# A four-layer graph network on one core: a new order of the stage of adj, ACT issuing a store, units of up to three chunks, and one norm from row sums

## The chip, the cores and the metric

The kernel runs on one core of a Trainium2 chip. The metric is the device time of one execution in microseconds (us). The engines are called PE (TensorE, matrix products), DVE (VectorE), ACT (ScalarE), POOL (GpSimd, which here gathers and scatters rows by DMA) and SP (SyncE, which here issues DMAs). Every engine has its own stream of instructions, in an order that is fixed when the kernel is built. Where an engine needs the result of another it waits on a semaphore, and everything behind the waiting instruction on that engine waits too.

## The reference

There are N = 3327 nodes with D = 512 features (x, fp32), and an adjacency matrix adj of 3327 x 3327 int32, in which about 0.12% of the entries are one: some four neighbours a row. Four layers follow, each of them x = x + layer(relu(norm(x))):

```python
# layer 0: mean over the neighbours
agg = mask @ h / max(deg, 1)
out = relu(concat(h @ W_self + b_self, agg @ W_nb + b_nb) @ W_comb + b_comb)
# layer 1: graph attention with 8 heads of 64
Wh = h @ W[head];  e = leaky_relu(f_src[i] + f_dst[j]), masked by adj
out = softmax(e) @ Wh
# layer 2: the same with 4 heads of 512/4 inputs expanded to quaternion weights, then elu
# layer 3: one head of 512:  out = softmax(e) @ (h @ W.T)
```

norm takes the mean and variance over the 512 features of a row, without learned scales.

## The kernel before, in words

The rows are handled in 26 chunks of 128 nodes. The kernel uses how sparse adj is: it builds a list of the neighbours of each row once, and each layer then gathers the rows of the neighbours from a table in DRAM. A general path without lists exists and is not taken with these inputs.

**Stage of adj** (lines 852 to 1513). SP loads adj in 52 halves of a chunk into four buffers (ai). DVE searches each half for its ones (FIND_INDEX, L1209), ACT counts them with a Square whose sum it keeps (L1217). In the same stage the weights are loaded; W_self and W_nb of layer 0 are multiplied with the halves of W_comb on PE (L976) and copied out as wf (L989 by ACT, L987 by DVE). The chunks of x are loaded, normed and turned (hT, copied by ACT at L1342), and two products per chunk follow (L1349): pz, the part that the neighbours will need, which ACT copies to zt (L1358, L1361) and SP stores to the table of layer 0 (L1366), and py, the part of the row itself. At the end the rows are sorted by their number of neighbours: 26 scatters of POOL (L1435) put the own rows into the sorted order, and a read brings back the sorted records (srec).

**Layers 0 to 3.** After the sort the chunks differ in how many neighbour slots they have: 14, 8, 7, 7, 6, 6, 6, 5, 5, 5, 5, 4 (five times), 3 (five times), 2 (three times), 1, 1 for chunks 0 to 25, 117 in all. For a chunk, POOL gathers one slot after the other (L1562, one indirect DMA of up to 128 rows) into a ring of 33 slots. Layer 0 sums the slots, on PE with an identity matrix (L1593) and on DVE (L1887, L1895); layers 1 and 2 compute attention weights (L1941 to L1978), multiply the slots with them on DVE (L2110) or, for as many slots as ON_ACT says, on ACT (L2096), and sum on PE and DVE (L2138). L2148 adds the result of layer 1 to xres, which stays in SBUF. Then `project` prepares the next layer for the same chunk: mean and variance (bn_stats and its aggregate on DVE, L1649 and L1650, or, where SUMMED is true, from row sums: the update at L2148 keeps the sum of its result, DVE turns it into a mean at L1617, ACT squares the centred row and keeps that sum at L1625), an inverse root (L822, L824 on ACT, L831 to L836 on DVE), relu on ACT (L1676), transposes on PE (L1694), copies on ACT (L1705), the product with the weights on PE (L1780; L1737 is a small additional one of layer 3), and copies out (L1803 to L1806), which SP stores to the next table (L1764, L1822). A next layer may gather only when the whole table is stored: POOL waits for it at a small memset, the mark (L2194). Layer 3 makes its products after the gathers: weighted sums on DVE (L2030), transposes (L2046), the product with W and the addition of xres on PE (L2060, L2058), a copy on ACT (L2067), and a scatter on POOL of the finished rows to the output (L2072), which stands in POOL's stream between the gathers.

**The order of the work.** The instructions of each engine are put in order when the kernel is built, by a list scheduler (class Plan). Every operation has an engine, a planned cost and a rank. The scheduler takes the operation that can start first by these planned costs and, where several can, the one with the lowest rank. `limits` gives the number of buffers of each kind that it may count on. In the stage of adj the rank follows the planned times that ORDER_W, WORK, WORK0, X0, X and SELF set (when the weights are due, when the chunk of x, and how late a chunk's py may be). In a layer the rank follows ORDERS: a tuple of units for each layer, each unit one or more chunks that share the small operations of norm and softmax. POOL gathers the units in this order.

```python
ORDERS = {
...
    3: (
        (0,), (7,), (17,), (15, 20), (25,), (11,), (3,), (23,), (1, 5), (24,), (4, 14), (16,), (12, 22), (8,),
        (9,), (10,), (18,), (2,), (13,), (19,), (21,), (6,),
    ),
}
ON_ACT = {
    1: {S: min(S // 3, 1) for S in range(1, SLOTS + 1)},
    2: {S: S // 5 for S in range(1, SLOTS + 1)},
}
SUMMED = {1: False, 2: False, 3: False}
```

Of the kernel before, what the change touches and what calls it, by code (L numbers as in the profile page):

```python
# [18 lines left out]
P = 128  # L19
# [7 lines left out]
def general_path(  # L27
# [519 lines left out]
    def l3_finish(pc, i, o):  # L547
# [15 lines left out]
SLOTS = 16  # L563
# [46 lines left out]
ORDER_W = {1: -20.0, 0: -1.0, "bias": -4.0, "later": 20.0}  # L610
ADJ, WORK, WORK0, X0, X, SELF = 1.0, 1.13, 1.2, -14.0, 1.77, 7.0
# [81 lines left out]
def gnn_stack_kernel(  # L693
# [41 lines left out]
    with ExitStack() as st:  # L735
# [82 lines left out]
        def rough(pool, tag, var, scale=1.0):  # L818

            n = var.shape[-1]  # L820
            ln = pool.tile([P, 2], F32, tag="ln", name=f"ln{tag}", bufs=3)[:, :n]
            nc.scalar.activation(ln, var, AF.Ln, bias=eps, scale=scale)  # L822
            r0 = pool.tile([P, 2], F32, tag="r0", name=f"r0{tag}", bufs=3)[:, :n]
            nc.scalar.activation(r0, ln, AF.Exp, bias=lift, scale=-0.5)  # L824
            return r0

        def refined(pool, tag, mv, r0):

            n = r0.shape[-1]
            a = pool.tile([P, 2], F32, tag="nra", name=f"nra{tag}", bufs=3)[:, :n]  # L830
            nc.vector.scalar_tensor_tensor(a, r0, -1.0, r0, ALU.mult, ALU.mult)  # L831
            nc.vector.scalar_tensor_tensor(a, mv[:, :, 1], EPS, a, ALU.add, ALU.mult)
            r = pool.tile([P, 2], F32, tag="rs", name=f"rs{tag}", bufs=3)[:, :n]
            nc.vector.scalar_tensor_tensor(r, a, 3.0 * LIFT * LIFT, r0, ALU.add, ALU.mult)
            nmr = pool.tile([P, 2], F32, tag="nmr", name=f"nmr{tag}", bufs=3)[:, :n]
            nc.vector.scalar_tensor_tensor(nmr, mv[:, :, 0], -1.0, r, ALU.mult, ALU.mult)  # L836
            return r, nmr

        def refined_sums(pool, tag, mv, r0):

            n = r0.shape[-1]
            a = pool.tile([P, 2], F32, tag="nra", name=f"nra{tag}", bufs=3)[:, :n]
            nc.vector.scalar_tensor_tensor(a, r0, -1.0 / D, r0, ALU.mult, ALU.mult)
            nc.vector.scalar_tensor_tensor(a, mv[:, :, 1], D * EPS, a, ALU.add, ALU.mult)
            r = pool.tile([P, 2], F32, tag="rs", name=f"rs{tag}", bufs=3)[:, :n]
            nc.vector.scalar_tensor_tensor(r, a, 3.0 * LIFT * LIFT, r0, ALU.add, ALU.mult)
            nmr = pool.tile([P, 2], F32, tag="nmr", name=f"nmr{tag}", bufs=3)[:, :n]
            nc.vector.tensor_tensor(nmr, mv[:, :, 0], r, ALU.mult)
            return r, nmr


        with tc.tile_pool(name="p0", bufs=1) as pa, tc.tile_pool(name="p0p", bufs=2, space=PSUM) as pp:
# [444 lines left out]
            for p0 in range(0, NK, 2):  # L1297
# [25 lines left out]
                for j, i in enumerate(unit):  # L1323
# [41 lines left out]
                    def store(i=i, key=key):  # L1365
                        nc.sync.dma_start(table[0][i * P : (i + 1) * P, :D], tiles["zt", key])  # L1366

                    rows_in.append(load(rank, 4.0 * P * D, store, (), [o2], give=("zt",)))
# [147 lines left out]
        with tc.tile_pool(name="run", bufs=1, reuse_waits="tile") as pr, tc.tile_pool(  # L1516
# [7 lines left out]
            limits = {"xy": 3, "acc": 2, "pt": 2, "pw": 2, "h": 3, "hT": 3, "t": 3, "neg": 2, "ee": 2, "y": 3}  # L1524
# [77 lines left out]
            def project(layer, unit, updated, rank):  # L1602
# [233 lines left out]
            def summing(layer, unit, j):  # L1836
# [3 lines left out]
                if j == 0:  # L1840
                    new("mv", (layer, unit[0]), [P, 2, 2])
# [418 lines left out]
```

## Time and profile before

| | |
|---|---|
| median of three runs | 1074.55 us (1073.38 to 1076.67) |
| profiled execution | 1231.77 us |
| its span | 1230.0 us |
| mean granted PE clock in it | 0.855 |
| busy in the span: PE, DVE, ACT, POOL | 901.8, 726.6, 518.2, 610.1 us |
| stage of adj, then sort | 0 to 268, 268 to 278 us |
| layer 0, 1, 2, 3 | 278 to 514, 514 to 759, 759 to 998, 998 to 1230 us |
| first and last gather, layer 0 | 278.2, 458.1 us |
| layer 1 | 518.6, 719.9 us |
| layer 2 | 763.8, 961.4 us |
| layer 3 | 999.3, 1201.5 us |

The profile is one execution on the chip taken by the hardware profiler; the median comes from other executions of the same program. The profiled one is 157 us longer than the median. "Busy" is time in which an engine executes; the loading of weights into PE overlaps its products and is counted apart (PEld). A line such as L1562 is a line of the kernel. A wait is written as the waiting instruction, an arrow, and the instruction that ended the wait, then the sum in us, the number of waits and the longest. The stages above are bounded by POOL's marks at 514.2, 759.5 and 998.4 us.

### The profile page before, as it was taken

The numbers are of one execution on the slowest core, as the hardware profiler recorded it, in microseconds if no ns is written. First come the engines' busy times: TensorE is split into PE (matmuls) and PEld (weight loads), VectorE is DVE, ScalarE is ACT, GpSimd is POOL, SyncE is SP. The second block draws the span as 40 slices with busy tenths as digits, with TensorE's granted clock in tenths as the row PEclk, the third lists the DMA queues.
The fourth block names the chain that finished last, engine by engine and source line by source line (L and its number), as shares of the span: only waits on it lengthen the run. The fifth ranks groups of instructions, "written<-read, shape, count | busy, mean of one in ns | idle before, by whom it ended". The sixth has DMA issues, their size and how long they took to land. (4 is left out here: it accounts for less than half of the span.)

```text
span 1230.0 us, 11605 instructions
## 1 busy us (share of the span) xinstructions
PE 901.8 (73%) x2853; PEld 510.4 (41%) x2853; DVE 726.6 (59%) x1848; ACT 518.2 (42%) x1700; POOL 610.1 (50%) x719
## 2 busy tenths in 40 slices
PE   7599999854098889752979796539979832948865
PEld 4244444322075656531647464214435421423322
DVE  6499989204176557453869784628894815534441
ACT  4488886210043433422656553316554621312221
POOL 1064246717655550175757511766883236675661
PEclk9899999977599899966989889659896956978987
DMA  9999894958587772265666521665754345575561
GB/s 352 338 364 338 294 306 146 317 203 286 172 268 252 247 249 89 76 195 149 198 183 178 154 79 55 189 187 150 209 169 129 91 121 149 168 206 160 163 186 59
DMA packets 89910, 240.49 MB, mean 196 GB/s; under 512 B 24933, under 2 KB 26477, under 8 KB 89834
## 3 DMA queue, kind: packets, MB, share of 16 engines
q0 software_dynamic: 41600, 137.72, 38.1%
q1 hardware_dynamic: 48234, 101.96, 23.3%
q8 instruction: 24, 0.39, 0.1%
q14 instruction: 52, 0.43, 0.1%
HBM read 190.35 MB, written 49.27 MB: 195 GB/s over the span
## 5 line engine op out<-in xcount | busy, mean ns | idle before, releaser
L1562 POOL DMA_INDIRECT ring<-table,nbr x351 | 368.5, 1050 | 185.5 <-issue 80.9
L1593 PE MATMUL acc<-ring,ident 128*128 128x512 f32 (+1 forms) x494 | 266.6, 676 | 66.8 <-DVE ring L2110 24.3
L1780 PE MATMUL pw<-w,hT 128*128 128x264 f32 (+1 forms) x832 | 197.3, 394 | 18.3 <-ACT hT L1705 13.6
L1780 PEld LDWEIGHTS pw<-w,hT 128*128 128x128 f32 x832 | 161.2, 195 | 60.9 <-ACT hT L1705 20.5
L1593 PEld LDWEIGHTS acc<-ring,ident 128*128 128x128 f32 (+1 forms) x494 | 98.7, 215 | 175.1 <-issue 107.5
L1562 POOL DMA_INDIRECT ring<-table,srec x117 | 110.1, 941 | 77.8 <-issue 31.5
L2110 DVE TENSOR_TENSOR ring<-ring,w 128x2048 f32<-128x2048 f32 (+7 forms) x76 | 114.3, 1531 | 4.7 <-DVE w L1978 3.0
L2060 PE MATMUL pw<-w,hT 128*128 128x512 f32 x208 | 101.7, 634 | 13.3 <-ACT hT L2052 11.0
L1209 DVE FIND_INDEX8 fidx<-one_i,ai 128x8 uint32<-128x832 int32 x104 | 104.2, 1018 | 0.0
L1349 PE MATMUL pz_n<-wf,hT_n 128*128 128x512 f32 x208 | 95.2, 609 | 10.9 <-ACT hT_n L1342 8.4
L1705 ACT ACTIVATE hT<-pt 128x128 f32<-128x128 f32 (+1 forms) x312 | 81.8, 292 | 39.7 <-PE pt L1694 18.5
L1217 ACT ACTIVATE junk<-ai 128x1664 int8<-128x1664 int32 (+1 forms) x52 | 82.7, 1590 | 32.6 <-DMA ai<-in_adj_dram 32.2
L1694 PE MATMUL pt<-ident,h 128*128 128x128 f32 x208 | 36.5, 312 | 75.9 <-ACT h L1676 73.4
L1349 PE MATMUL py_n<-wf,hT_n 128*128 128x512 f32 x208 | 91.9, 592 | 0.0
L1803 ACT COPY t<-pw 128x512 f32<-128x512 f32 (+1 forms) x54 | 30.6, 566 | 134.0 <-PE pw L1780 43.9
L1941 DVE TENSOR_TENSOR e<-ring,fs 128x24 f32<-128x24 f32 (+25 forms) x96 | 15.2, 172 | 120.2 <-DMA ring<-table,nbr 102.0
L2060 PEld LDWEIGHTS pw<-w,hT 128*128 128x128 f32 x208 | 42.3, 207 | 73.2 <-issue 51.3
L1705 ACT ACTIVATION_READ_ACCUMULATOR hT<-pt 128x1 f32 x312 | 69.5, 223 | 0.0
L1694 PEld LDWEIGHTS pt<-ident,h 128*128 128x128 f32 x208 | 28.1, 160 | 96.3 <-ACT h L1676 81.6
L2194 POOL MEMSET mark<- 1x1 f32 x3 | 0.3, 88 | 132.7 <-DMA table<-t 132.7
L1349 PEld LDWEIGHTS pz_n<-wf,hT_n 128*128 128x128 f32 x208 | 39.8, 195 | 62.8 <-issue 49.4
L2046 PE MATMUL pt<-ident,y 128*128 128x128 f32 x96 | 16.4, 312 | 67.4 <-issue 56.8
(185 smaller groups left out, 1319.7 us busy)
## 6 DMA issues: line engine op xcount, KB each, us to landing
ai<-in_adj_dram SPq DMA_DIRECT2D x25, 832.0 KB
ai<-in_adj_dram SPq DMA_DIRECT2D x25, 831.5 KB
table<-t SPq DMA_DIRECT2D x52, 258.0 KB
xy<-own SPq DMA_DIRECT2D x26, 512.0 KB
table<-t SPq DMA_DIRECT2D x26, 260.0 KB
table<-zt_n SPq DMA_DIRECT2D x26, 256.0 KB
ring<-table,nbr POOLq DMA_INDIRECT x351
later<-in_x_dram SPq DMA_DIRECT2D x15, 256.0 KB
```

What stands on the lines that cost most here:

```text
L1209: nc.vector.max_index(fidx[:, i, qq * 8 : (qq + 1) * 8], one_i, ai[:, q * QW : min(cols, (q + 1) * QW)])
L1217: nc.scalar.activation(junk[:, :cols], tiles["ai", key][:, :cols], AF.Square, accum_out=sq[:, i, hf : hf + 1])
L1349: nc.tensor.matmul(pz, tiles["hT", key][:, c, :], wf[s][:, c, :], start=(c == 0), stop=(c == DC - 1))
L1562: nc.gpsimd.indirect_dma_start(out=ring[:m, r0 + s, : width[layer]], out_offset=None, in_=table[layer], in_offset=bass.IndirectOffsetOnAxi ...
L1593: nc.tensor.matmul(acc, ident[:m, :], g[:m, s, :D], start=(k == 0), stop=(k == len(slots) - 1))
L1694: nc.tensor.transpose(pt[:, c, :], h[:, c * P : (c + 1) * P], ident)
L1705: nc.scalar.activation(hT[:, c, :n], pt[:, c, :n], AF.Copy, accum_out=hsum[layer][:, i, c : c + 1])
L1780: nc.tensor.matmul(pw[:, b, :w], tiles["hT", key][:, c, :], wsb[layer][:, c, b, :w], start=(c == 0), stop=(c == DC - 1),)
L1803: nc.scalar.copy(t[:, :D].rearrange("p (b f) -> p b f", b=2)[:, lo:hi, :], pw[:, lo:hi, :HD])
L2046: nc.tensor.transpose(pt[:, c, :], tiles["y", key][:, c * P : (c + 1) * P], ident)
L2060: nc.tensor.matmul(pw[:, 0, :], tiles["hT", key][:, c, :], w3[:, c, :], start=False, stop=(c == DC - 1))
L2110: nc.vector.tensor_tensor(v, v, box["w"][:m, j, lo:hi, :].unsqueeze(3).to_broadcast([m, hi - lo, H, O]), ALU.mult,)
```

## The change

All of it changes the order of the work or the engine that does it; what is computed stays.

- The store of zt to the table of layer 0 is issued by ACT instead of SP (26 stores); the plan counts 0.35 us of ACT for it. ORDER_W, WORK, WORK0, X0, X and SELF have new values, and the plan counts 1.5 instead of 2.0 us for the landing of each scatter of the own rows. In the resulting order of SP ten chunks of x instead of eight are loaded ahead of W_self, and W of layer 3 before the third half of adj.
- ORDERS is new for all layers. Layers 0 to 3 had 22, 19, 19 and 22 units of one or two chunks and have 23, 22, 18 and 18 of one to three. Small tiles shared by a unit have three columns instead of two.
- The rules of ON_ACT for layers 1 and 2 are exchanged: layer 1 multiplies 12 slots on ACT instead of 21, layer 2 21 instead of 12.
- SUMMED is true for layer 2. That norm is computed in the stage of layer 1: 26 bn_stats with their aggregates leave DVE, 22 small centring operations come to it, the 26 updates of L2148 keep a sum, and ACT gains 26 Squares that keep a sum.
- The scheduler counts on one buffer instead of two for neg and two instead of three for y.

```diff
 ORDERS = {
     0: (
-        (24,), (12, 21), (11,), (6,), (18,), (17,), (15,), (4,), (3,), (20,), (5, 9), (22,), (10, 19), (1,),
-        (2,), (14,), (0,), (23,), (8,), (13, 16), (7,), (25,),
+        (9,), (20,), (17,), (24,), (8,), (11, 18, 22), (0,), (4,), (23,), (3,), (13,), (12, 15), (5,), (6,),
+        (10,), (1,), (7,), (14,), (2,), (21,), (19,), (16,), (25,),
     ),
     1: (
-        (18, 21), (22, 24), (15,), (5,), (10, 20), (2,), (17,), (12, 23), (19,), (4,), (9, 14), (7,), (11, 16),
-        (8, 13), (6,), (1,), (0,), (3,), (25,),
+        (22,), (10,), (15,), (24,), (20,), (12,), (5,), (17,), (4, 9), (14, 18), (13, 16), (23,), (6,), (7,),
+        (21,), (2,), (11, 19), (0,), (8,), (3,), (1,), (25,),
     ),
     2: (
-        (18, 23), (19, 24), (16,), (20,), (6, 11), (10, 14), (7, 12), (5, 13), (9,), (1,), (21, 22), (4,), (0,),
-        (8,), (2,), (3,), (15,), (17,), (25,),
+        (21,), (16, 24), (22,), (9, 17, 19), (12,), (2,), (23,), (11, 14), (15, 20), (5,), (4, 7, 13), (6, 8),
+        (0,), (1,), (3,), (18,), (10,), (25,),
     ),
     3: (
-        (0,), (7,), (17,), (15, 20), (25,), (11,), (3,), (23,), (1, 5), (24,), (4, 14), (16,), (12, 22), (8,),
-        (9,), (10,), (18,), (2,), (13,), (19,), (21,), (6,),
+        (20, 25), (22,), (11, 23), (9, 13, 18), (12, 19), (7,), (15, 17), (14,), (2,), (8,), (1, 3, 4), (24,),
+        (16,), (21,), (0,), (6,), (5,), (10,),
     ),
 }
 ON_ACT = {
-    1: {S: min(S // 3, 1) for S in range(1, SLOTS + 1)},
-    2: {S: S // 5 for S in range(1, SLOTS + 1)},
+    1: {S: S // 5 for S in range(1, SLOTS + 1)},
+    2: {S: min(S // 3, 1) for S in range(1, SLOTS + 1)},
 }
-SUMMED = {1: False, 2: False, 3: False}
+SUMMED = {1: False, 2: True, 3: False}
...
-ORDER_W = {1: -20.0, 0: -1.0, "bias": -4.0, "later": 20.0}
-ADJ, WORK, WORK0, X0, X, SELF = 1.0, 1.13, 1.2, -14.0, 1.77, 7.0
+ORDER_W = {1: -37.41, 0: -0.2, "bias": -17.46, "later": 14.56}
+ADJ, WORK, WORK0, X0, X, SELF = 1.0, 1.18, 0.3, -20.32, 2.18, 4.08
...
                     def store(i=i, key=key):
-                        nc.sync.dma_start(table[0][i * P : (i + 1) * P, :D], tiles["zt", key])
-
-                    rows_in.append(load(rank, 4.0 * P * D, store, (), [o2], give=("zt",)))
+                        nc.scalar.dma_start(table[0][i * P : (i + 1) * P, :D], tiles["zt", key])
+
+
+                    o2 = put("act", 0.35, rank, store, (), [o2])
+                    rows_in.append(plan.add("dma", 4.0 * P * D / 370e3, rank, None, [o2], lag=2.0, give=("zt",)))
...
-                landed.append(plan.add("dma", 2.0, (-1.0, pos), None, [o], lag=1.5))
+                landed.append(plan.add("dma", 1.5, (-1.0, pos), None, [o], lag=1.5))
...
-            limits = {"xy": 3, "acc": 2, "pt": 2, "pw": 2, "h": 3, "hT": 3, "t": 3, "neg": 2, "ee": 2, "y": 3}
+            limits = {"xy": 3, "acc": 2, "pt": 2, "pw": 2, "h": 3, "hT": 3, "t": 3, "neg": 1, "ee": 2, "y": 2}
...
-                                norm["mv"] = new("mv", (layer, unit[0]), [P, 2, 2])
+                                norm["mv"] = new("mv", (layer, unit[0]), [P, 3, 2])
```

More of the change, by code (lines that the diff above doesn't have):

```diff
@@ L820, in rough @@
             n = var.shape[-1]
-            ln = pool.tile([P, 2], F32, tag="ln", name=f"ln{tag}", bufs=3)[:, :n]
+            ln = pool.tile([P, 3], F32, tag="ln", name=f"ln{tag}", bufs=3)[:, :n]
             nc.scalar.activation(ln, var, AF.Ln, bias=eps, scale=scale)
-            r0 = pool.tile([P, 2], F32, tag="r0", name=f"r0{tag}", bufs=3)[:, :n]
+            r0 = pool.tile([P, 3], F32, tag="r0", name=f"r0{tag}", bufs=3)[:, :n]
             nc.scalar.activation(r0, ln, AF.Exp, bias=lift, scale=-0.5)
@@ L829, in refined @@
             n = r0.shape[-1]
-            a = pool.tile([P, 2], F32, tag="nra", name=f"nra{tag}", bufs=3)[:, :n]
+            a = pool.tile([P, 3], F32, tag="nra", name=f"nra{tag}", bufs=3)[:, :n]
             nc.vector.scalar_tensor_tensor(a, r0, -1.0, r0, ALU.mult, ALU.mult)
             nc.vector.scalar_tensor_tensor(a, mv[:, :, 1], EPS, a, ALU.add, ALU.mult)
-            r = pool.tile([P, 2], F32, tag="rs", name=f"rs{tag}", bufs=3)[:, :n]
+            r = pool.tile([P, 3], F32, tag="rs", name=f"rs{tag}", bufs=3)[:, :n]
             nc.vector.scalar_tensor_tensor(r, a, 3.0 * LIFT * LIFT, r0, ALU.add, ALU.mult)
-            nmr = pool.tile([P, 2], F32, tag="nmr", name=f"nmr{tag}", bufs=3)[:, :n]
+            nmr = pool.tile([P, 3], F32, tag="nmr", name=f"nmr{tag}", bufs=3)[:, :n]
             nc.vector.scalar_tensor_tensor(nmr, mv[:, :, 0], -1.0, r, ALU.mult, ALU.mult)
@@ L841, in refined_sums @@
             n = r0.shape[-1]
-            a = pool.tile([P, 2], F32, tag="nra", name=f"nra{tag}", bufs=3)[:, :n]
+            a = pool.tile([P, 3], F32, tag="nra", name=f"nra{tag}", bufs=3)[:, :n]
             nc.vector.scalar_tensor_tensor(a, r0, -1.0 / D, r0, ALU.mult, ALU.mult)
             nc.vector.scalar_tensor_tensor(a, mv[:, :, 1], D * EPS, a, ALU.add, ALU.mult)
-            r = pool.tile([P, 2], F32, tag="rs", name=f"rs{tag}", bufs=3)[:, :n]
+            r = pool.tile([P, 3], F32, tag="rs", name=f"rs{tag}", bufs=3)[:, :n]
             nc.vector.scalar_tensor_tensor(r, a, 3.0 * LIFT * LIFT, r0, ALU.add, ALU.mult)
-            nmr = pool.tile([P, 2], F32, tag="nmr", name=f"nmr{tag}", bufs=3)[:, :n]
+            nmr = pool.tile([P, 3], F32, tag="nmr", name=f"nmr{tag}", bufs=3)[:, :n]
             nc.vector.tensor_tensor(nmr, mv[:, :, 0], r, ALU.mult)
@@ L1840, in summing @@
                 if j == 0:
-                    new("mv", (layer, unit[0]), [P, 2, 2])
+                    new("mv", (layer, unit[0]), [P, 3, 2])
                 return {"accum_out": tiles["mv", (layer, unit[0])][:, j, 0:1]}
```

## The prediction

> **What bounds the kernel now.** I read the page first (engine shares, slices, groups), then a table of busy time by stage, the chains of waits in each stage, and the instruction timeline at the stage heads. No engine carries the whole:
>
> ```profile
> span 1230.0 us, 11605 instructions
> PE 901.8 (73%) x2853; PEld 510.4 (41%) x2853; DVE 726.6 (59%) x1848; ACT 518.2 (42%) x1700; POOL 610.1 (50%) x719
> ```
>
> TensorE leads with 901.8 us, but a quarter of the span is not TensorE. The view by stage (stage of adj, sort, layers 0 to 3) shows where:
>
> ```profile
> core 0: us, PE busy (x) PEld busy (x) DVE busy (x) ACT busy (x) POOL busy (x), PEclk, DMA share, GB/s
> 0.00:268.00 268.00, 234.03 (x639) 110.37 (x639) 186.44 (x517) 161.89 (x261) 104.00 (x221) 0.96 0.83 299
> ...
> 514.00:759.00 245.00, 180.97 (x652) 121.84 (x651) 165.93 (x397) 119.27 (x539) 124.02 (x118) 0.85 0.51 149
> 759.00:998.00 239.00, 172.54 (x550) 93.81 (x548) 151.47 (x374) 110.60 (x449) 134.12 (x118) 0.78 0.52 153
> 998.00:1220.00 222.00, 140.40 (x364) 65.50 (x364) 91.37 (x252) 47.59 (x96) 136.86 (x144) 0.81 0.55 163
> ```
>
> The stage of adj is TensorE's: 234 of 268 us, and the 34 missing are 6.5 at the start and seven gaps. Of these one of 10.3 us waits for a folded weight (ACT's copy of wf), one of 7.7 for hT near the end. A layer is instead a stream with two ends. Until the first unit has its rows TensorE has nothing; then gathers come 1.25 us apart (below: 518.65, 519.90), (0.95 + 0.30), so the 117 of a layer need 117 × 1.25 = 146 us; after the last gather comes a tail, because TensorE has fallen behind. Last gathers are at 458.1, 719.9, 961.4 and 1201.5, so the tails to the next stage (or the end) last 56.1, 39.6, 37.1 and 28.5 us.
>
> ```profile
> 518.65 0.95 POOL L1562 DMA_INDIRECT ring<-table,nbr  x1 [4.36 <-DMA table<-t]
> 519.90 0.94 POOL L1562 DMA_INDIRECT ring<-table,nbr  x1 [0.30 <-issue]
> 530.81 3.78 PE L1593 MATMUL acc<-ring,ident 128*128 128x512 f32 x4 [15.96 <-issue]
> 1030.43 1.12 PE L2046 MATMUL pt<-ident,y 128*128 128x128 f32 x4 [35.13 <-issue]
> ```
>
> The square brackets give the idle time before: TensorE stands 16.0 us at the head of layer 1, 16.5 at that of layer 2 and 35.1 at that of layer 3. The last is what layer 3's first unit costs: chunk 0, with 14 slots. Layer 3's other wait is POOL's: it scatters outputs between gathers and is held by ACT's copy.
>
> ```profile
> POOL out_dram L2072 <- ACT t L2067: 37.1, 10, 5.9
> POOL mark L2194 <- DMA table<-t: 132.7, 3, 56.1
> PE pt L1694 <- ACT h L1676: 35.8, 8, 18.1
> SPq L1366 <- ACT zt_n L1358: 34.5, 12, 9.8
> ```
>
> The second line says that POOL stands 132.7 us in three waits for the stores that end layers 0 to 2, which are the tails; the third (layer 1's window) that TensorE waits there for relu; the fourth (stage of adj) that SP's queue stands 34.5 us in front of the stores of zt.
>
> The profiled execution took 1231.77 us (span 1230.0) against a median of 1074.55, 157 us more. It has long stretches in which several engines idle together. I make the sums on its durations, and put the resulting difference on the median; anything measured by long idle is therefore discounted.
>
> **What the Trainium skill says.** "DMA: Bandwidth & Descriptors", section "Issuing engines are not separate DMA queues": issuing from another engine saves only issue time, since the transfers share the same 16 DMA engines. The trace has 0.32 us for an issue of SP, and the share of 0.83 in the stage of adj says that transfers don't gain. "TensorE: Matmul & The Clock Gate", "HAM oscillation — how this bites in real kernels": idle gaps lower TensorE's clock. The trace agrees: the granted clock is 0.5 from 41.4 after the gap at 38.4, and from 246.2 after that at 243.6. So a shorter head is worth a little more than its length. "ScalarE: Activation LUTs", "Table sets: the hidden batching unit": changing functions may reload a table. The trace has one load (1.28 us) although Square, Ln, Exp and copies alternate, so new Squares should add none. "VectorE: DVE Perf Modes", "Two Vector instructions with no wait between them": an operation with an accumulator output is two instructions. No such VectorE operation was read in the trace of before; ACT's accumulator read takes 0.19.
>
> **The change part by part.**
>
> *Stores of zt by ACT.* SP loses 26 × 0.32 = 8.3 us of issue and its waits of 34.5 + 10.2 us for zt, so loads of adj behind them may start earlier. ACT gains 26 issues, by SP's price 8.3 us (0.2 to 0.6 each: 5 to 16). ACT makes zt itself, so no wait for another engine is added; behind the issue stand the Squares that count adj and the copies of hT. ACT is busy 161.9 of 268, which hides 8.3; uncovered it is 8.3. SP's loads also wait for the search to free a buffer of adj (58.7 us in 29 waits), which stays.
>
> *New order of the stage.* Ten chunks of x instead of eight go ahead of W_self, W of layer 3 comes earlier. On ACT the first copy of wf moves ahead of the counting of adj's third chunk; but the third copy comes behind the counting of the fourth, and VectorE's copy behind two more searches of 1.02 each. The gap of 10.3 is moved more than removed; the last eight products of the stage stay in the same order. Ends: 10.3 + 3 us gained with smaller gaps, against +6 if a weight is late. I take −3.
>
> *Units.* Slots of the first unit, after against before: layer 0 5 for 1, layers 1 and 2 2 for 5, layer 3 4 for 14. At 1.25 a slot: +5.0, −3.75, −3.75, −12.5. But the head is not the layer. A bound for each: the largest, over units, of 1.25 × slots gathered up to the unit plus TensorE's work from it on. Per chunk that work is 3.7 for a projection (layer 1's share of the row of L1780, 96.5 us over 26), 0.66 for transposes (36.5 over 52, a little less at a full clock), 5.1 + 0.66 in layer 3 (rows of L2060, L2058 and L2046), and per slot summed on PE 1.08 (row of L1593, 266.6 over 247), or an estimated 0.86 where the clock is full. With 0.86 the bound goes from 175.0 to 177.8 (layer 0), 176.0 to 173.3 (1), 160.3 to 160.3 (2), 169.2 to 157.6 (3); with 1.08 the differences are +3.0, −2.9, +2.2 and −11.6. So: layer 0 +3, layer 1 −3, layer 2 −1 (its head of −3.75 half repaid by the stream).
> In layer 3 POOL issues 117 × 1.25 + 26 × 1.31 = 180 us of the 222 (a scatter lasts 1.0 and is followed by 0.3). In its old order the first scatter stands behind 32 gathers and in the new behind 14: 18 × 1.25 = 22.5 us earlier. Seven chunks are still open behind gather 107 or later instead of ten. Of the ends 0 and −22.5 I take −10, because the flow bound gives −11.6 and ten outputs × 5.1 of TensorE stay near the end. In that layer a unit of three chunks holds 21 of 33 ring slots, so that chunk 0 behind it has 12 to look ahead. Layer 2 of before has the same look-ahead at one place, where POOL stood 15.0 us (935 to 950).
>
> *Norm from row sums, in the stage of layer 1.* VectorE loses 26 × (0.69 + 0.18) = 22.6 (rows of L1649 and L1650), and gains 22 × 0.17 = 3.7 for centring (one a unit, by the small operations of L831 to L836). ACT gains 26 Squares with accumulator at 0.63 + 0.19 = 0.82 (the row of L1142, same shape): 21.3. The accumulator output on the update has no row: 0 to 0.2 × 26; I take 2. The chain to relu changes by −0.87 + 0.17 + 0.82 = +0.12 for a unit of one chunk and +0.94 for one of two, as the Squares aren't split over engines: 18 × 0.12 + 4 × 0.94 = 5.9 if all of it shows. VectorE's relief hides it; I take 0.
>
> *Rule for ACT's products swapped.* Layer 1 goes from 21 slots on ACT to 12: ACT −72 × 0.268 = −19.3 (row of L2096: 57.8 over 216, eight operations a slot), VectorE +9 × 0.58 = +5.2 (row of L2110: 114.3 over 197 slots). With the norm: VectorE −22.6 + 3.7 + 5.2 + 2 = −11.7 of 165.9, ACT +2.0 of 119.3. Layer 2 the other way: ACT +9.6 of 110.6, VectorE −5.2 of 151.5. TensorE (181.0 and 172.5) lies over both, and covers it; I take 0. Limits neg 2 to 1 and y 3 to 2 bound the planned order only.
>
> Sum: −3 + 3 − 3 − 1 − 10 + 0 = −14 us; 1231.8 − 14 = 1218 profiled, and on the median 1074.5 − 14 = **1060.5**.
>
> **Rivals.** *Gains stack* (0.20): the gap of adj goes (−13), both heads show whole (−7.5), layer 3 gives 22. Then 1074.5 − 42.5 = 1032. For it: a head leaves TensorE idle on a chain that nothing else carries. Against: tails say that TensorE is behind afterwards, and an earlier start then shortens only what it is short of.
> *It only moves the idle* (0.09): the heads are taken from slack, layer 3 stays at POOL's 180 + waits, layer 0's +3 cancels the rest: 1071 to 1078. For it: a layer's sum of TensorE work is unchanged.
> *Slower* (0.26): the 26 Squares of 0.82 stand on ACT directly ahead of the relus for which TensorE already waits 35.8 us in layer 1. If all 21.3 show and layer 1's 3 are lost: 1074.5 − 11 + 21.3 = 1085. It decides once some 14 of the 21.3 show. For it: relu is named as the releaser of TensorE's longest waits there. Against: ACT loses 72 products in that same stage.
>
> **How the numbers follow.** Likeliest (0.45): 1043 to 1071, its own range around 1060.5. Stacked: 1020 to 1043. Moved only: 1071 to 1078. Slower: 1078 to 1105. A range of 1030 to 1088 leaves out some 0.08 below and 0.10 above. A measurement of this kernel tells about 0.3% (3.2 us) from no change; faster 0.65, within 0.09, slower 0.26.
>
> **What would show it.** Right: TensorE's idle at the head of layer 3 falls from 35 towards 15 to 20 us, those of 1 and 2 to about 12; the wait of the scatter for ACT's t falls below 30 and the stretch of layer 3 below 215; SP's waits for zt are gone, the adj stage is within 5 us of 268. Wrong: TensorE's wait for relu in layer 1 above 50 us; a new TensorE gap over 10 us in the stage of adj with wf as releaser; a POOL stall of 15 us or more in layer 3 at chunk 0 behind the unit of three.

## The result

The changed kernel takes 1082.39 us (median of five, 1081.27 to 1084.52) where the kernel before takes 1073.38 (1072.78 to 1076.67): a ratio of 1.0069, 95% interval 1.0045 to 1.0093. It is slower by 0.7%, where 1060.5 and "faster" were forecast. The time lies inside the range, on the wrong side of no change.

The profile of before on which the prediction was built was an execution of 1231.77 us. The kernel before was therefore profiled once more, unchanged, and this execution took 1075.54 us. All readings of before in this part are from that second profile, unless said otherwise. Some runs further down, marked with a dagger, were on chips on which the kernel before itself takes 1219 to 1236 us, with waits that the profile gives no cause for; each ratio is against before on the same chip. A ratio takes the executions of each kernel within 1.5% of its own fastest, and as these are only 20 of 57, 15 of 27 and 22 of 27 executions of before on the three chips with a dagger, the ratio of the medians of all stands beside it there.

The pages of both, before first and then the changed kernel:

```profile
span 1073.5 us, 11605 instructions
PE 874.7 (81%) x2853; PEld 496.5 (46%) x2853; DVE 725.1 (68%) x1848; ACT 518.5 (48%) x1700; POOL 621.8 (58%) x719
```

```profile
span 1079.5 us, 11579 instructions
PE 871.0 (81%) x2853; PEld 491.5 (46%) x2853; DVE 706.5 (65%) x1846; ACT 534.6 (50%) x1720; POOL 625.7 (58%) x719
```

DVE loses 18.6 us of work and ACT gains 16.1, where the ledger's sums for layers 1 and 2 are −16.9 and +11.6; the span grows by 6.0. Where it grows is in the view of busy time by stretch. The stretches are cut at the first gather of each layer: up to it, then layers 0, 1, 2, 3. Before:

```profile
core 0: us, PE busy (x) PEld busy (x) DVE busy (x) ACT busy (x) POOL busy (x), PEclk, DMA share, GB/s
0.00:266.70 266.70, 232.18 (x639) 110.00 (x639) 187.03 (x520) 163.07 (x263) 105.12 (x223) 0.95 0.87 308
266.70:450.90 184.20, 167.95 (x654) 114.72 (x654) 130.51 (x305) 78.73 (x359) 110.63 (x119) 0.97 0.80 268
450.90:655.90 205.00, 169.78 (x650) 116.77 (x650) 164.88 (x397) 118.93 (x539) 128.56 (x118) 0.93 0.63 178
655.90:870.10 214.20, 171.88 (x546) 92.97 (x546) 150.92 (x374) 110.30 (x443) 140.31 (x118) 0.80 0.60 169
870.10:1073.50 203.40, 132.90 (x364) 62.04 (x364) 91.74 (x252) 47.48 (x96) 137.19 (x143) 0.84 0.62 178
```

The changed kernel:

```profile
0.00:271.10 271.10, 232.98 (x639) 111.23 (x639) 185.75 (x520) 164.90 (x263) 105.43 (x223) 0.94 0.86 303
271.10:453.60 182.50, 168.04 (x654) 114.35 (x654) 130.59 (x309) 78.72 (x361) 111.30 (x118) 0.97 0.82 271
453.60:667.00 213.40, 171.53 (x650) 117.01 (x650) 155.94 (x416) 123.78 (x527) 134.30 (x118) 0.93 0.59 171
667.00:874.30 207.30, 162.91 (x546) 86.43 (x546) 144.98 (x364) 119.61 (x476) 136.71 (x118) 0.85 0.61 175
874.30:1079.50 205.20, 135.51 (x364) 62.46 (x364) 89.25 (x237) 47.62 (x93) 137.94 (x143) 0.84 0.60 176
```

Up to the first gather +4.4, layer 0 −1.7, layer 1 +8.4, layer 2 −6.9, layer 3 +1.8: together +6.0. In layer 1 TensorE works 1.7 us more and stands 6.7 us more; in the stage of adj its work is the same within 0.8. In layer 2 it works 9.0 us less, for the same 546 products, and stands 2.1 us more; the granted clock there (PEclk) is 0.85 instead of 0.80. All of these are single executions: layer 3 took 203.2 to 204.7 us in five profiles of that chip in which its order is the one of before, and 208.9 in a sixth (two_layers, below). A difference of one or two us between two profiles therefore says little.

The heads that the prediction wanted to shorten were shortened. TensorE's first work in layer 1 came after 15.72 us of idle before, and after 11.74 now; in layer 3 it was 35.53 and is 13.27. Timeline of the changed kernel, the square brackets giving the idle time ahead:

```profile
461.56 2.07 PE L1595 MATMUL acc<-ring,ident 128*128 128x512 f32 x2 [11.74 <-DVE ring L2112]
580.84 5.76 PE L1782 MATMUL pw<-w,hT 128*128 128x260 f32 x16 [7.29 <-ACT hT L1707]
601.03 2.54 PE L1782 MATMUL pw<-w,hT 128*128 128x260 f32 x5 [4.90 <-ACT hT L1707]
883.73 1.11 PE L2048 MATMUL pt<-ident,y 128*128 128x128 f32 x4 [13.27 <-DVE y L2032]
1007.95 1.12 PE L2048 MATMUL pt<-ident,y 128*128 128x128 f32 x4 [27.92 <-DVE y L2032]
```

The first and fourth lines are these heads; the others are the other half of the story. In layer 1 two new gaps appear in front of projections, and in layer 3 a gap of 27.92 us lies behind the unit of three chunks, whose 21 slots take 21 × 1.25 = 26 us to gather. All of TensorE's idle time in layer 3 is 69.7 us, against 70.5 before.

### The profile page after: what moved, and what is told of

Same layout as the page of the kernel before. It is cut to its first block, busy times and chain, and to the rows that moved or that the text cites. A ratio compares the mean times of both kernels' runs of the same rounds, so it can differ in the third digit from the quotient of the medians.

```text
span 1079.5 us, 11579 instructions
## 1 busy us (share of the span) xinstructions
PE 871.0 (81%) x2853; PEld 491.5 (46%) x2853; DVE 706.5 (65%) x1846; ACT 534.6 (50%) x1720; POOL 625.7 (58%) x719
## 5 line engine op out<-in xcount | busy, mean ns | idle before, releaser
L1564 POOL DMA_INDIRECT ring<-table,nbr x351 | 382.4, 1089 | 118.7 <-issue 66.2
L1595 PE MATMUL acc<-ring,ident 128*128 128x512 f32 (+1 forms) x494 | 252.8, 645 | 65.6 <-DVE ring L2112 43.4
L1782 PEld LDWEIGHTS pw<-w,hT 128*128 128x128 f32 x832 | 160.0, 194 | 58.0 <-ACT hT L1707 22.7
L1595 PEld LDWEIGHTS acc<-ring,ident 128*128 128x128 f32 (+1 forms) x494 | 92.1, 203 | 170.8 <-issue 73.9
L1943 DVE TENSOR_TENSOR e<-ring,fs 128x16 f32<-128x16 f32 (+22 forms) x96 | 15.6, 174 | 155.8 <-DMA ring<-table,nbr 151.8
L2112 DVE TENSOR_TENSOR ring<-ring,w 128x1024 f32<-128x1024 f32 (+6 forms) x76 | 114.8, 1532 | 1.7
L1349 PE MATMUL pz_n<-wf,hT_n 128*128 128x512 f32 x208 | 92.0, 593 | 0.0
L1707 ACT ACTIVATE hT<-pt 128x128 f32<-128x128 f32 (+1 forms) x312 | 82.0, 291 | 19.0 <-PE pt L1696 18.4
L1970 ACT ACTIVATE ex<-el 128x8 f32<-128x8 f32 (+22 forms) x54 | 12.2, 227 | 122.0 <-DVE el L1953 121.4
L2062 PEld LDWEIGHTS pw<-w,hT 128*128 128x128 f32 x208 | 40.7, 200 | 61.9 <-issue 46.3
L2032 DVE SCALAR_TENSOR_TENSOR acc<-ring,w,acc 128x512 f32<-128x512 f32 (+2 forms) x67 | 50.5, 754 | 14.6 <-ACT acc L2030 13.0
L1349 PEld LDWEIGHTS py_n<-wf,hT_n 128*128 128x128 f32 x208 | 38.9, 193 | 43.4 <-issue 43.2
```

The costliest lines, as they stand in the source:

```text
L1349: nc.tensor.matmul(pz, tiles["hT", key][:, c, :], wf[s][:, c, :], start=(c == 0), stop=(c == DC - 1))
L1564: nc.gpsimd.indirect_dma_start(out=ring[:m, r0 + s, : width[layer]], out_offset=None, in_=table[layer], in_offset=bass.IndirectOffsetOnAxi ...
L1595: nc.tensor.matmul(acc, ident[:m, :], g[:m, s, :D], start=(k == 0), stop=(k == len(slots) - 1))
L1707: nc.scalar.activation(hT[:, c, :n], pt[:, c, :n], AF.Copy, accum_out=hsum[layer][:, i, c : c + 1])
L1782: nc.tensor.matmul(pw[:, b, :w], tiles["hT", key][:, c, :], wsb[layer][:, c, b, :w], start=(c == 0), stop=(c == DC - 1),)
L1943: nc.vector.tensor_tensor(e[:m, j, lo:hi, :], g[i][:m, lo:hi, D : D + H], fsrc[layer][:m, i, :].unsqueeze(1).to_broadcast([m, hi - lo, H]) ...
```

## The experiments

The times that follow are medians; "layer 1" and so on are the stretches just shown, from the profile of the run.

**The kernel before, unchanged.** 

> The kernel before, unchanged, to have a profile whose time is near its median. All theories: ratio 1.000 within 0.3%, profiled span near 1072 us. If the 157 us by which the first profile of before was longer were a property of profiling, this one would again be near 1230. If they were a disturbance of that one execution, the stages should come out near 262, 178 to 190, 210, 210 and 205 us.

1076.34 us against 1076.5, ratio 0.9997 (0.998 to 1.0015); span 1073.5. So the 157 us belong to that one execution and not to profiling as such. Which chip it ran on is not on record; on the three chips with a dagger the kernel before is as slow as that. In the second profile POOL's wait for ACT's copies in layer 3 is 11.9 us in 4 waits, where the prediction read 37.1 in 10, and the gathers of all layers follow one another with hardly a wait.

**The stage of adj alone.**

```diff
-ORDER_W = {1: -20.0, 0: -1.0, "bias": -4.0, "later": 20.0}
-ADJ, WORK, WORK0, X0, X, SELF = 1.0, 1.13, 1.2, -14.0, 1.77, 7.0
+ORDER_W = {1: -37.41, 0: -0.2, "bias": -17.46, "later": 14.56}
+ADJ, WORK, WORK0, X0, X, SELF = 1.0, 1.18, 0.3, -20.32, 2.18, 4.08
...
-nc.sync.dma_start(table[0][i * P : (i + 1) * P, :D], tiles["zt", key])
+nc.scalar.dma_start(table[0][i * P : (i + 1) * P, :D], tiles["zt", key])
```

> Before with only the part of the stage of adj: stores of zt issued by ACT, the new ORDER_W, WORK, WORK0, X0, X and SELF, and the landing of 1.5. Adj theory (the new order of the stage makes a weight late, the gap is repeated): +5 to +10 us. Norm theory and units theory: -3 us as in the prediction, between -10 and +2.

1081.69, ratio 1.0048 (1.0029 to 1.0068), first gather at 276.2 instead of 266.7; the layers keep their lengths within 1.3 us. The profiled execution is 4 us above the run's median, so the 9.5 us of the profile overstate a loss that is 5.2 in the medians. The adj theory was right. Waits of TensorE in the stage, this kernel and then before:

```profile
PE pm_w L976 <- DVE wf L987: 14.7, 1, 14.7
PE pt_n L1337 <- ACT h_n L1328: 8.2, 1, 8.2
```

```profile
PE pm_w L976 <- ACT wf L989: 10.7, 1, 10.7
PE pm_w L976 <- DVE wf L987: 1.7, 1, 1.7
```

Both kernels have a hole of some 14 us in which no half of adj has landed. Before, ACT's copy of wf stood behind one counting Square when the next half came. Now it is DVE's copy that is last, behind the searches of two more halves (at 48.5 and 51.2 us in the changed kernel; the copy ends at 53.9). The second gap is new: h of a chunk is late because ACT's first small operation for it stands behind Squares of halves for which ACT idles 7.1 and 1.7 us in the changed kernel.

**The two parts of it.** First the new times alone†: 

> Before with only the new ORDER_W, WORK, WORK0, X0, X and SELF; the stores of zt stay on SP. Weights theory (the new order of loads puts DVE's copy of wf behind one more half of adj, and h of a later chunk behind late halves): the gaps of 14.7 and 6 to 8 us on PE are there again and the run is 4 to 10 us slower. Store theory (ACT's issues delay what stands behind them): within 2 us of before, one gap of 10.7.

Ratio 1.0056 (1.0023 to 1.0089), of the medians 1.0024; a gap of 16.3 us for DVE's wf, then 5.5 and 3.9 in front of products. The first gather is at 279.2, where two runs with the old stage on the same chip have 275.1 and 274.0. Then the stores alone: 

> Before with only the stores of zt issued by ACT (26 of them), the old times and order otherwise. Weights theory (the new times make the loss): the gaps on PE stay one of about 10.7 and small ones, and the run is within 3 us of before or up to 3 us faster. Store theory (the issues on ACT make it): 4 to 6 us slower, with the gap near 176 us in the stage.

1075.65 against 1076.29, ratio 1.0004 (0.9983 to 1.0025), first gather at 266.9. TensorE's first gap is again ACT's:

```profile
PE pm_w L976 <- ACT wf L989: 10.4, 1, 10.4
PE pm_tot L1408 <- DVE ai_sort L1396: 3.4, 1, 3.4
```

So the 26 issues on ACT cost nothing that can be measured (the interval reaches from −1.8 to +2.7 us), and SP's 80 us of waits in front of those stores (70.0 and 10.2 in before) bought nothing when they went: SP's queue then waits for the search to free a buffer (81.6 us instead of 60.5). What is left as the loss is the order of weights and halves of adj; the planned 1.5 us for a landing was not run alone.

**The old stage in the changed kernel†.** 

> The changed kernel with the old stage of adj (old times, stores on SP, landing 2.0). Weights theory: first gather at 267 instead of 271, one PE gap of about 10.7 in the stage, the run 4 to 6 us faster than the changed kernel, about 1077. Rival (the old stage costs as much elsewhere, layer 0 is fed later): within 2 us of the changed kernel.

Ratio 0.999 (0.9962 to 1.0017) to before, of the medians 0.9969. There is no run of the changed kernel on that chip, so this says only that without the stage's edits the rest is not slower there: layer 1, all new, takes 229.0 in its profile, and 232.2 all old in another on that chip (rule2_only).

**The new units alone.** Only ORDERS, the tiles of three columns and the limits. 

> Before with only the new ORDERS of all four layers, tiles of three columns and the limits of neg and y. Units theory (units of three chunks make the chains longer and the first unit of layer 0 later): +5 to +12 us, most of it in layers 0 and 2. Norm theory: -8 us, as in the prediction, layer 3 shorter by about 10 us. Adj theory: -8 us too.

1099.01, ratio 1.0199 (1.0165 to 1.0232). Layer 1 takes 225.8 (+20.8), layer 2 218.0 (+3.8), layer 0 181.7 (−2.5), layer 3 205.8 (+2.4). The loss is not in layers 0 and 2 as the units theory put it, but in layer 1. Layer 3, which the norm theory had about 10 us shorter, gains nothing. Units and limits were not run apart.

**The norm alone.**

```diff
-SUMMED = {1: False, 2: False, 3: False}
+SUMMED = {1: False, 2: True, 3: False}
```

> Before with only the norm of layer 2 from row sums (SUMMED true for layer 2). Norm theory (26 Squares of 0.82 us on ACT stand directly ahead of the relus for which PE waits): +10 to +21 us, all of it in the stage of layer 1. Units theory and adj theory: between -4 and +3 us, since DVE is relieved of 22.6 us.

1084.22, ratio 1.0066 (1.0044 to 1.0087); layer 1 213.0 (+8.0). (In both kernels with this norm and the old units, the tile of the sums is made by whichever chunk of a unit comes first.) The layer grew by 8.0 net, less than the norm theory's 10 to 21. Of these, 3.3 us are longer work of TensorE and 4.7 idle time, and TensorE's waits for relu, by which the theory explained its loss, fell from 7.8 to 6.1 us. A Square with its read takes 0.73 + 0.20, more than the 0.82 forecast; the read of the accumulator on DVE takes 0.08, less than the 0.2 allowed for.

**The rules of ON_ACT alone.** First†: 

> Before with only the exchanged rules of ON_ACT. Prediction's ledger: 0 in both layers, since TensorE lies over both. Gather theory (a product of DVE holds up the gather that runs beside it, and gathers are the stream that feeds a layer): layer 1 with nine more slots on DVE has gathers that take about 5 us more in sum and is 3 to 6 us longer; layer 2 with nine fewer has 4 us less and is 3 to 5 us shorter; the sum is within 2 us of nothing.

Ratio 1.023 (1.0156 to 1.0305), of the medians 1.0152. Once more, where before runs at 1076: 

> The exchange of ON_ACT alone once more, because the first look was taken where the kernel before itself ran at 1222 us with stalls of all engines that hide single stages. Gather theory: layer 1 is 3 to 6 us longer than 205 and layer 2 3 to 5 us shorter than 218, in sum within 2 us of nothing. If the units planned for the old rule don't fit the new one: both layers longer, 10 to 25 us in sum, as the 2.3% of the first look says.

1084.44, ratio 1.0077 (1.0047 to 1.0107). Layer 1 takes 217.2 (+12.2), layer 2 209.1 (−5.1). Layer 2 moved as the gather theory said; layer 1 moved at least twice as far, so neither theory holds whole. The groups of layer 1's gathers, before and in this run (busy, mean ns of one, then idle ahead):

```profile
L1562 POOL DMA_INDIRECT ring<-table,nbr x117 | 128.5, 1098 | 39.7 <-issue 17.7 <-DMA ring<-table,nbr 5.8 <-DMA table<-t 4.4
L2110 DVE TENSOR_TENSOR ring<-ring,w 128x2048 f32<-128x2048 f32 (+7 forms) x38 | 54.7, 1469 | 0.4
```

```profile
L1562 POOL DMA_INDIRECT ring<-table,nbr x117 | 134.7, 1151 | 39.7 <-issue 18.6 <-DMA ring<-table,nbr 7.0 <-DMA table<-t 4.4
L2110 DVE TENSOR_TENSOR ring<-ring,w 128x2048 f32<-128x2048 f32 (+7 forms) x38 | 59.8, 1596 | 0.6
```

The same 117 gathers take 6.2 us longer when DVE multiplies nine more slots. In layer 2, with nine fewer, they fall from 140.2 to 133.8. A gather that runs alone takes 0.95. That long gathers are DVE's doing the next run shows. The number of slots is not all that sets their sum: with the old rule and the new units (orders_only) the sums are 133.6 and 136.7. Nor are gathers all of the +12.2: TensorE works 6.9 us more in that layer (176.66, at a granted clock of 0.89 instead of 0.93), and its waits for DVE's products are 33.4 us instead of 22.4.

**All products of layer 2 on ACT†.**

```diff
-    2: {S: S // 5 for S in range(1, SLOTS + 1)},
+    2: {S: S for S in range(1, SLOTS + 1)},
```

> Before with all products of layer 2 on ACT, none on DVE: a measurement of what slows gathers, not a version to keep, since ACT gets some 103 x 4 x 0.27 = 110 us more. Gather theory (DVE's products hold the gathers up): the 24 gathers above 1.1 us in layer 2 fall to 3 or fewer and the sum of all 117 from 140 to about 112 us, though the layer gets 15 to 50 us longer. Rival (transfers or the table's rows are slow in layer 2): as many slow gathers as before, sum near 140.

One execution of 1283.26 against 1221.79; layer 2 takes 304.3 us, 73.5 more than with the old rule on that chip (adj_times_only), where 15 to 50 were expected. Groups of layer 2 in it:

```profile
L2096 ACT ACTIVATE ring<-ring,w 128x128 f32<-128x128 f32 (+3 forms) x460 | 140.2, 396 | 0.7 <-issue 0.7
L1562 POOL DMA_INDIRECT ring<-table,nbr x117 | 110.1, 941 | 119.3 <-PE acc L1593 82.9 <-issue 15.8 <-DVE xres L2178 8.4
```

Not one gather is above 1.1 us, and the sum is 110.1; layers 0 and 3 have 110.1 to 111.7 in every run. The rival (slow rows or transfers) is gone. The timeline of the changed kernel shows the holding itself, POOL and then DVE:

```profile
513.66 0.95 POOL L1564 DMA_INDIRECT ring<-table,nbr  x1 [0.30 <-DMA ring<-table,nbr]
514.92 2.23 POOL L1564 DMA_INDIRECT ring<-table,nbr  x1 [0.30 <-DMA ring<-table,nbr]
517.45 0.96 POOL L1564 DMA_INDIRECT ring<-table,nbr  x1 [0.30 <-issue]
```

```profile
514.02 2.29 DVE L2112 TENSOR_TENSOR ring<-ring,w 128x2048 f32<-128x2048 f32 x1
```

The gather that began at 513.66, before the product, takes 0.95. The one begun at 514.92, while the product runs, ends at 517.15, 0.84 after the product's end at 516.31. This is the rule in the whole second profile of before. Of its 44 long gathers in layers 1 and 2, 43 begin while a product of L2110 runs, and 39 of these end 0.82 or 0.83 us after the end of that product; the last one begins while L2178 adds two SBUF tiles. Twelve more gathers begin in a product and are not long: two within 0.01 us of its start, the others in its last 0.27. The 30 gathers into which a product starts take 1.0 or less, and so do 89 in all layers that begin at least 0.3 us before the end of a DVE operation with one input in PSUM.

The Trainium skill, "SBUF — State Buffer", section "Who interferes with whom", says that a DVE instruction with both inputs in SBUF contends with a GpSimd instruction that reads SBUF. Gathers read their lists in SBUF, and L2110's inputs are both there; the sums of L1887 and L2138 have one input in PSUM, and layers 0 and 3 have no slow gather. So far numbers and page agree. The same section infers that such a product does not stall the making of a DMA's descriptors; here it holds indirect gathers, and the measurement decides.

**The norm undone in the changed kernel.** First†: 

> The changed kernel with the norm of layer 2 from bn_stats again; all else as changed. Norm theory (the Squares cost what they cost alone): 7 to 8 us faster than the changed kernel, so about 1074, layer 1 near 205. Order theory (the new order of layer 1 costs 21 us with the old norm, and the new norm takes part of that back): slower than the changed kernel, 1086 to 1095, layer 1 between 218 and 226.

Ratio 1.02 (1.014 to 1.0259), of the medians 1.0146. Once more: 

> The changed kernel with the norm of layer 2 from bn_stats once more, for the same reason. Norm theory: near 1074, layer 1 near 205. Order theory (the units of layer 1 were laid for the new norm; with the old one they cost 10 to 20 us): 1090 to 1100, layer 1 between 220 and 230.

1101.22, ratio 1.024 (1.0205 to 1.0275); layer 1 takes 231.8. The order theory had the direction, and the loss came out a little above its ranges. With the new units and the new rule the norm gives back 18.4 us of layer 1, though on the old ones it cost 8.0. One sees where in POOL's timeline of this run:

```profile
624.26 0.96 POOL L1564 DMA_INDIRECT ring<-table,nbr  x1 [0.30 <-DVE den L1978]
637.49 0.92 POOL L1564 DMA_INDIRECT ring<-table,nbr  x1 [12.27 <-PE acc L1595]
```

Towards the end of the new order stand chunks 0, 8, 3 and 1 with 14, 5, 7 and 8 slots, 34 in all. The ring of 33 is full, and POOL waits 12.27 us for TensorE to sum slots that DVE has only just multiplied. In the changed kernel, with 22.6 us of bn_stats gone from DVE, the longest stall of a gather in the layer after its first is 2.6.

**Single edits of layer 1 undone in the changed kernel†.** 

> The changed kernel with the old rule of ON_ACT for layer 1 (21 slots on ACT instead of 12). Gather theory (nine slots fewer on DVE, shorter gathers): gathers of layer 1 about 5 us less in sum, layer 1 3 to 6 us shorter than 213, run near 1077. Fit theory (units, rule and norm of layer 1 were laid out together, each one undone costs): layer 1 220 or more, run 1088 or more.

> The changed kernel with the old units of layer 1; rule and norm as changed. Units theory (the new units of layer 1 are the loss): layer 1 205 to 208 us, run near 1075. Fit theory: layer 1 215 to 225, as the old units with either the norm or the rule alone gave 213 and 217; run 1083 to 1092.

The old rule: 1.0056 (1.0024 to 1.0088), of the medians 1.0022, and on another chip, as 

> The changed kernel with the old rule of ON_ACT for layer 1, once more. Gather theory: sum of the gathers of layer 1 about 5 us less than 134, layer 1 3 to 6 us shorter than 213, run 1076 to 1079. Fit theory: layer 1 220 or more, run 1088 or more. The first look (1.0056 of before) lies nearer to no change against the changed kernel.

0.9952 (0.9925 to 0.9979), of the medians 0.9935. The old units: 1.0338 (1.0262 to 1.0413), of the medians 1.0322, layer 1 254.7. The nearest kernel on that chip is the one with all of layer 1 new and the old stage of adj: 1215.54 against 1258.5, layer 1 229.0. The stage of adj accounts for some 5 of these 43 us. So the new units are not what one would take out: with the new norm and rule the old ones are worse. On the rule the two runs differ in sign, and neither was where before runs at 1074; it stays open.

**Only what gained.** New units of layers 0 and 2, and the rule of layer 2: 

> Before with the new units of layers 0 and 2 and the new ON_ACT rule of layer 2 alone; the stage of adj, layers 1 and 3 and the norm stay. By the two undisturbed profiles layer 0 was 1.6 us and layer 2 6.9 us shorter in the changed kernel. Additive theory (a layer's stretch belongs to its own order): -6 to -9 us against before, faster than both kernels, near 1066. Interaction theory (layer 2 gained because layer 1 left it another state): -2 to +3 us.

1082.14, ratio 1.0057 (1.0037 to 1.0078): neither theory, as the loss is above what the interaction theory allowed. Layer 0 gave its 2.2, layer 2 only 1.1 (213.1), and layer 1, whose units, rule and norm are those of before, took 214.6 instead of 205.0. Its instructions on TensorE, DVE and ACT stand in another order, because one plan lays out all four layers (2 to 5% of them have moved), and its gathers take 133.1 instead of 128.5. But the profiled execution, 1088.55, is the slowest of the run's thirteen, 6.4 us above the median, and layer 3, in which no instruction changed its place, takes 208.9 in it instead of 203.4. How much of the 9.6 us of layer 1 belongs to the order, and how much to that execution, is not shown. Then the rule of layer 2 alone†: 

> Before with only layer 2's rule of ON_ACT (21 slots on ACT instead of 12). Gather theory: gathers of layer 2 about 6 us less in sum (140 to 134), layer 2 4 to 6 us shorter, layer 1 as before, run 1068 to 1072, faster than both kernels. Fit theory (layer 1's order moves with it): layer 1 longer by 5 to 10, run 1075 to 1080.

1.0201 (1.0159 to 1.0242), of the medians 1.0101, and again† 

> Before with only layer 2's rule of ON_ACT, once more. Gather theory: sum of the gathers of layer 2 falls from 140 to about 134, layer 2 is 4 to 6 us shorter and layer 1 as before, run 1068 to 1072, faster than both kernels. Fit theory: layer 1 longer by 5 to 10, or layer 2 held by the copies of ACT, run 1075 or more.

1.0128 (1.0077 to 1.018), of the medians 1.0095. Here the gathers of layer 2 are short (124.6 and 125.7), yet POOL stands long in front of ring slots that ACT's neg (L2164) has not released, 41.6 us in the first of the two (the line counts one gather of layer 3 too). Where before runs at 1076, the same rule had layer 2 5.1 us shorter (onact_again); the rule of layer 2 was not run alone there. The gain of the gather theory did not come, and the hold by ACT that the second expectation named did.

```profile
L1562 POOL DMA_INDIRECT ring<-table,nbr x118 | 125.6, 1064 | 99.1 <-ACT neg L2164 41.6 <-issue 28.3 <-DMA table<-t 10.6
```

No version tried was shown to be faster than before in more than one run.

## Why the prediction was wrong

The sum said −14, the profiles say +6. Against the forecast the stage of adj is 7.4 us worse, layer 1 11.4 and layer 3 11.8; layers 0 and 2 are 4.7 and 5.9 better. That the time stayed inside the range is owed to these last two, without which it would be near 1093. Nothing in the sum foresaw them, so this was luck.

**The stage of adj (−3 taken, +4.4 in the profile, +0.5% alone).** The failing step is the choice between two named ends, "10.3 + 3 us gained with smaller gaps, against +6 if a weight is late". The late weight was found by reading the order (DVE's copy behind two more searches) and then given no weight of its own. Its price was 14.7 − 10.7 = 4.0 on this gap (3.3 over all waits of L976, 15.7 instead of 12.4); the second gap, 6.2 in the changed kernel, was not seen. Of the signs named for "wrong" this one came (a gap over 10 us with wf as releaser); the other two did not. The signs named for "right" in the layers came as well: heads of 11.7, 12.1 and 13.3 us, a wait of the scatter of 13.2, a layer 3 of 205. They could not tell right from wrong, because the second profile of before already has 11.9 and 203 for the last two. "More moved than removed" was right, and moved work had to be priced at the landing of the later half. The stores were costed at nothing and cost nothing.

**Layer 3 (−10 taken, +1.8).** The head is 22.3 us shorter, more than the 12.5 worked for it. The step "half of 22.5" failed because the layer is bound by POOL's stream: 176.2 us from first to last gather before, 178.4 now, against 117 × 1.25 + 22 or 23 scatters × 1.3 = 175 or 176. The prediction had such a number (180) and set it against a stretch of 222, read from a window that ended 10 us ahead of the disturbed layer's end, which made POOL look as if it had 40 us to spare; in the undisturbed profile the stream of gathers and scatters has next to none. What TensorE no longer waits at the head it waits at 27.92 behind the unit of 21 slots. In every run on the faster chip the layer takes 203 to 209 us, with either set of units; that POOL's stream sets it is read from the traces, no run moved it.

**Layer 1 (−3 taken, +8.4).** The head fell by 4.0, as worked. What failed is "TensorE lies over both, and covers it; I take 0", for the norm and the rule. Work counts said ACT +2 and DVE −12, and +4.9 and −8.9 came; the larger change is in when an in-order engine reaches its next instruction. With nine more slots on DVE and another order, whose shares no run parts here, the gathers slip: at the 61st gather of the layer the stream lags 13.2 us behind a pace of 1.25, against 6.2 before. Around 572 us DVE stands for a late gather (3.80, then 2.42), ACT stands behind it at the exponential, and the copies of hT for which TensorE waits are queued behind that and behind a Square of the new norm, which waits 2.00 us more:

```profile
572.53 0.19 DVE L1943 TENSOR_TENSOR e<-ring,fs 128x32 f32<-128x32 f32 x1 [3.80 <-DMA ring<-table,nbr]
575.15 0.18 DVE L1943 TENSOR_TENSOR e<-ring,fs 128x24 f32<-128x24 f32 x1 [2.42 <-DMA ring<-table,nbr]
```

```profile
576.19 0.26 ACT L1970 ACTIVATE ex<-el 128x64 f32<-128x64 f32 x1 [7.18 <-DVE el L1953]
578.45 0.72 ACT L1627 ACTIVATE junk<-xres,mv 128x512 bf16<-128x512 f32 x1 [2.00 <-DVE mv L1619]
580.39 0.30 ACT L1707 ACTIVATE hT<-pt 128x128 f32<-128x128 f32 x1
```

TensorE's waits for hT in the layer are 14.4 us instead of 1.4, those for relu 8.2 instead of 7.8, and those for DVE's products 16.3 instead of 22.4. The slower rival named the right layer and the wrong wait: relu hardly waits longer; a Square does stand in the chain shown, in front of hT. Alone the norm costs 8; in the changed kernel taking it out costs 18 more. The gap of 7.29 us costs more than its length: the clock granted from 578.1 to 584.8 is 0.50, and of the 16 products behind the gap the first nine start some 0.43 us apart and the others 0.22. They take 5.76 us, where the next 16 of the same line, at a clock of 1.00, take 3.67:

```profile
589.45 3.67 PE L1782 MATMUL pw<-w,hT 128*128 128x260 f32 x16
```

**Layers 0 and 2 (+3 and −1 taken, −1.7 and −6.9).** Layer 0's first unit of five slots showed nothing of its 5 us: TensorE began 4.4 us after the first gather in both kernels, as it sums slots one by one as they land, and then had no gap above 1.5 us. In layer 2 the head shrank (16.7 to 12.1) and the gathers took 3.7 us less, a term that was not in the sum at all; nine slots left DVE, but the new units alone had the gathers 3.5 us shorter and the layer 3.8 longer, so the two are not parted. The gain stands in TensorE's busy time, 9.0 us less at a higher granted clock, and not in its idle time, which grew by 2.1. Whether the clock or the waits inside the stream of products made it was not tested.

**What was wrong in the reading.** 157 us of the first profile were discounted as idle, but its waits were still used as sizes: the 37.1 us of POOL for ACT's copies (11.9 undisturbed), the 35.8 of TensorE for relu (7.8), the tails of 56 to 28 us (37 to 27). The page of the first profile has a mean of 1050 ns for a gather of layers 1 to 3 (L1562), where the prediction's own lines have single ones of 0.95 and 0.94; the difference was not asked about.

## What to carry to other kernels

Look for the mean of a repeated instruction that is longer than one of its kind alone: here 0.95 grew to between 1.10 and 1.20, only in the layers where DVE multiplies SBUF tiles by SBUF tiles, and such work on DVE holds the very stream that feeds it. Where all engines run in an order fixed beforehand, edits of a plan don't add: three edits that cost 8, 12 and 21 us alone in one layer cost 8 together, and a layer whose own edits were taken out still had some of its instructions in other places and was no longer what it had been. A profile of an execution that is 15% above the median shows the order of things, not their sizes; take another before summing.

## What the hardware showed that was not expected

An indirect gather on POOL that begins while DVE works on two inputs in SBUF is held until that operation ends, and ends 0.82 us after it; one that began earlier is not held. In before 20 of 117 gathers in layer 1 and 24 in layer 2 took 1.2 to 3.6 us instead of 0.95, 17.7 and 29.7 us more in all, and none did when ACT made the products. The kernel before took 1070 to 1085 us on one chip and 1198 to 1244 on three others, with the same number of gathers and DMA packets. In the first profile, which was as slow, ACT stands up to 30.8 us in front of copies out of PSUM for which the trace shows nothing that it waits for. What makes these waits was not found.
